# A fixed order for VectorE in the first strip, the weight quantised earlier, the second strip's keys and gates moved

## The chip, the cores and the metric

The kernel runs on one core of a Trainium2 chip. A core has a matrix engine (TensorE, PE), a vector engine (VectorE, DVE), an engine for functions such as exp (ScalarE, ACT), a general one (GpSimd, POOL) and one that only issues transfers and waits (SyncE, SP). Each runs its own queue strictly from front to back; an instruction that waits for a semaphore holds up all that is queued behind it. Tiles lie in SBUF (128 partitions), results of matmuls in PSUM. The metric is the device time of one execution in microseconds (us): less is better.

## What is computed

Two layers over 2 x 2048 tokens of 256 features. Layer 0, which the change touches, adds to x a gated linear attention with two heads and a linear map whose activations and weight are rounded to a six-bit grid in blocks of 32:

```python
xn = _layernorm(x)
v, q, lg = jnp.split(xn @ W_in.T, 3, axis=-1)
q = silu(q); k = 1.0 - sigmoid(lg); g = log_sigmoid(lg)
# per head, token by token:  S = exp(g)[:, None] * S + k[:, None] * v[None, :];  o = q @ S
o = o * sigmoid(xn @ W_g1.T @ W_g2.T)
attn = (o - mean(o)) * rsqrt(var(o) + 1e-5) * ln_w @ W_out.T
ffn = dequantised(xn) @ dequantised(weight).T + bias
x = x + attn + ffn
```

Layer 1 is an attention with 16 heads and a routed mixture of eight experts; its part of the program (some three quarters of the time) has almost the same order before and after.

## The kernel before

Layer 0 (`layer0`, L499 on) goes over the tokens in eight strips of 512, each held as four tiles of 128 tokens; strips 0 to 3 and 4 to 7 are the two sequences. A `Strip` has one method for each piece of work:

- `norm_x`: statistics (`LayerNorm.see`: `bn_stats` L119, `bn_aggr` L121), then `LayerNorm.apply`: the variance plus eps (L126), a power on GpSimd (L128), four scalings to `xn` (L130). GpSimd then adds the feed-forward bias to x (L613). There is one buffer of `xn` (`bufs=1`).
- `columns_x`: eight transposes on TensorE (L565) and two ScalarE copies to `xnT`.
- `values_gates`: `vf_ps` on TensorE (four tiles), for each a VectorE copy to `logit` (L633) and a ScalarE copy to `v` (L634), and for two tiles at a time `soft`, in two ScalarE steps.
- `queries`: `q_ps` and the cumulative gates `c_ps` on TensorE, `ls` on ScalarE, `arg` and `q` on VectorE (L680 to L683). `keys` (`k_ps`, `kt`), `gates` (`g1T`), `gates_end` (`gate`), `key_columns` (`k_tr`, `k`).
- `quantise`: the rounding of `xn`, in two halves of two tiles. Each half runs `mx_steps` (L149): nine operations on VectorE and then GpSimd (L191), VectorE (L193), GpSimd (L194), VectorE (L196), GpSimd (L197), each on the result of the one before. `quantised_columns` transposes the result (`mx_v` to `xdT`). `quantised_weight` does the same once for the weight `ffnw`, with four transposes (`wtr`).
- `weights` (`a_ps`, masked by VectorE at L757), then `chunk(0)` to `chunk(3)`: `o_ds_ps` on TensorE, the running state on VectorE and ScalarE (`sum` L796, `state` L799, `to_next` L792), `og` and its statistics.
- `norm_o`, `columns_o`, `sum_up` (`y_ps`), `norm_2`, `columns_2`, and `queries_keys`, `values`, `greatest` for the next layer.

The pieces of neighbouring strips are interleaved by hand in the loop at the end of `layer0` (L867 on): while strip s goes through its chunks, strip s+1 gets its values, queries, keys and gates, and strip s+2 is normalised.

The written order binds TensorE: every matmul and transpose of layer 0 goes through `tc.keep_in_program_order`, and instructions given to it stay on their engine in the order in which they were written. All others are placed by a scheduler at build time, among the pinned ones, by its own idea of when they are ready. On VectorE only two steps of `mx_steps` (L193, L196) are pinned, and for the weight none.

PSUM has six tiles under the name `mm` that `vf_ps`, `q_ps`, `c_ps`, `k_ps`, `g_ps`, `tr` and others share. SP issues the loads of x and constants in the written order, each also waiting until one of eight semaphores is free again; ScalarE's queue issues the loads of `wvf`, `wqT`, `sums`, `wg1T`, `wg2T` at the start.

## Time and profile before

Four runs have a median of 1774.44 us (1773.37 to 1775.82). One execution was profiled.

| | us |
|---|---|
| profiled execution, its own time | 1774.15 |
| its span in the profile | 1772.3 |
| TensorE busy | 1674.6 (94%) |
| VectorE busy | 694.4 (39%) |
| ScalarE busy | 803.4 (45%) |
| GpSimd busy | 395.8 (22%) |

The starts of `vf_ps`, the first matmuls of a strip's values, cut layer 0 into stages: 19.73 us for strip 0, then 48.76, 105.90, 156.97, 207.08, 256.4, 308.2 and 358.3. Attention begins at 453.8.

How to read the lines that follow. A row of the timeline has start, duration, engine, source line, operation, output and inputs, shapes, a count where several were merged, and in brackets how long the engine sat idle before it and what ended that. A row of waits has who waited, for whom, the total in us, how often, and the longest. A row of windows gives a stretch, its length, the busy time and number of instructions for TensorE's matmuls, its weight loads, VectorE, ScalarE and GpSimd, then the granted share of TensorE's clock, the share of the DMA engines and GB/s. A line number can be that of a helper: L565 are all transposes, L515 all matmuls of layer 0.

### The profile page before, as it was taken

What the parts mean: (1) busy time and instruction counts of PE and PEld (TensorE: products, weight loads), DVE (VectorE), ACT (ScalarE), POOL (GpSimd) and SP (SyncE); (2) the same over time, 40 slices, a digit from 0 to 9 for tenths busy, and PEclk for the clock granted to TensorE, in tenths of its full rate; (3) what the DMA queues carried; (4) which work ended last, traced back from release to release, by engine and by line L of the source; (5) the groups of instructions that cost most, each with busy time, mean ns of one, the idle gap of its engine ahead of it and who ended that gap; (6) DMA issues with size and microseconds to landing.
All of it is one profiled execution on the core that took longest, in us unless ns stands there. A gap on an engine that the chain in (4) does not pass through costs nothing.

```text
span 1772.3 us, 31816 instructions
## 1 busy us (share of the span) xinstructions
PE 1674.6 (94%) x13314; PEld 1298.1 (73%) x13314; DVE 694.4 (39%) x1798; ACT 803.4 (45%) x1590; POOL 395.8 (22%) x350
## 2 busy tenths in 40 slices
PE   5789999998999989999999999999999999999995
PEld 2467666666666656766666688898888888889885
DVE  7877767654554663242242222222222222222221
ACT  2345554453787767978988911111111111111110
POOL 4332222121200003333320012222222222222211
PEclk9899999999999999999999999999999999999998
DMA  9601113104610401351130175556555556557531
GB/s 250 171 23 39 50 50 91 59 24 104 139 13 1 77 13 60 90 116 60 54 136 14 38 271 172 164 174 214 177 179 185 183 183 195 164 176 238 164 84 17
DMA packets 82505, 204.33 MB, mean 115 GB/s; under 512 B 8624, under 2 KB 64304, under 8 KB 71728
## 3 DMA queue, kind: packets, MB, share of 16 engines
q0 software_dynamic: 24944, 138.33, 24.3%
q1 hardware_dynamic: 56304, 62.71, 13.7%
q8 instruction: 106, 1.74, 0.4%
q10 hardware_dynamic: 1104, 1.18, 0.2%
q14 instruction: 47, 0.39, 0.1%
HBM read 152.26 MB, written 49.92 MB: 114 GB/s over the span
## 4 chain that ended last, share of the span: by engine, by line
PE 82%; DVE 9%; ACT 5%; POOL 1%; DMA 1%; issue 1%; SPq 0%; POOLq 0%; DVEq 0%
PE h_ps L2113 27%; PE y_ps L2129 13%; PE sc L1687 11%; PE o_ps L1718 10%; PE qk_ps L515 3%; ACT pt L1693 3%; PE y_ps L515 3%; PE vf_ps L515 2%; PE f_ps L1670 2%; DVE pt L1705 2%; PE tr L565 2%; PE vg_ps L515 2%; PE g_ps L515 2%; PE o_tr L1644 1%; PE o_ds_ps L515 1%; PE x_ps L2091 1%
## 5 line engine op out<-in xcount | busy, mean ns | idle before, releaser
L1693 ACT ACTIVATE pt<-sc,shift 128x512 f32<-128x512 f32 (+3 forms) x832 | 463.9, 680 | 98.7 <-PE sc L1687 96.7
L2113 PE MATMUL h_ps<-va,qk 128*128 128x256 f32 (+1 forms) x2368 | 484.3, 365 | 0.0
L2113 PEld LDWEIGHTS h_ps<-va,qk 128*128 128x128 f32 x2368 | 425.4, 190 | 53.3 <-ACT va L2095 0.2
L2118 ACT ACTIVATE sg<-h_ps 128x256 f32<-128x256 f32 (+1 forms) x296 | 109.1, 369 | 593.8 <-PE h_ps L2113 575.9
L1687 PE MATMUL sc<-qk 32*128 32x256 f32 (+6 forms) x3680 | 276.4, 369 | 4.2 <-DVE onT L1664 1.7
L2119 DVE TENSOR_TENSOR larger<-sg,h_ps 128x256 f32<-128x256 f32 (+1 forms) x296 | 119.2, 403 | 355.4 <-ACT sg L2118 336.2
L1687 PEld LDWEIGHTS sc<-qk 32*128 32x128 f32 x3680 | 201.0, 185 | 62.8 <-ACT pt L1693 26.9
L1718 PE MATMUL o_ps<-pt,va 128*32 128x256 f32 (+7 forms) x3680 | 229.3, 352 | 17.5 <-DVE o_sb L1751 17.4
L1718 PEld LDWEIGHTS o_ps<-pt,va 128*32 128x32 f32 x3680 | 122.2, 110 | 96.9 <-issue 29.6
L2138 POOL DMA_INDIRECT out<-va,to x69 | 110.1, 1595 | 214.3 <-DVE larger L2119 59.3
L1705 DVE TENSOR_TENSOR pt<-pt,keepmask 128x1024 f32<-128x1024 f32 x64 | 78.3, 1224 | 184.8 <-ACT pt L1693 184.8
L2129 PE MATMUL y_ps<-qk,larger 128*128 128x256 f32 x560 | 124.3, 379 | 1.0 <-DVE va L2134 1.0
L2129 PE MATMUL y_ps<-larger 128*128 128x256 f32 x544 | 120.4, 379 | 0.0
L2129 PEld LDWEIGHTS y_ps<-qk,larger 128*128 128x128 f32 x560 | 104.8, 190 | 14.8 <-DVE va L2134 1.4
L2134 DVE SCALAR_TENSOR_TENSOR va<-y_ps,wt,half_bias 128x256 f32<-128x256 f32 x69 | 30.5, 480 | 209.8 <-PE y_ps L2129 209.8
L2129 PEld LDWEIGHTS y_ps<-larger 128*128 128x128 f32 x544 | 102.0, 190 | 13.1
L2023 POOL DMA_INDIRECT table<-rows,place x64 | 69.7, 1089 | 185.2 <-DMA table<-rows,place 147.1
L2053 POOL DMA_INDIRECT qk<-in_wgateup,wrow x37 | 37.3, 1009 | 284.1 <-PE h_ps L2113 150.3
L515 PE MATMUL vf_ps<-qk,xnT 128*128 128x512 f32 x128 | 58.8, 614 | 0.0
L515 PE MATMUL o_ds_ps<-state,q 128*128 128x128 f32 x120 | 26.1, 301 | 22.8 <-ACT state L799 22.8
L515 PEld LDWEIGHTS vf_ps<-qk,xnT 128*128 128x128 f32 x128 | 24.3, 195 | 29.3 <-issue 27.3
L1675 DVE TENSOR_TENSOR acc<-acc,f_ps 128x512 f32<-128x512 f32 x32 | 22.0, 687 | 56.8 <-PE f_ps L1670 54.1
(246 smaller groups left out, 1722.6 us busy)
## 6 DMA issues: line engine op xcount, KB each, us to landing
xb<-table SPq DMA_DIRECT2D x32, 265.0 KB
qk<-qk SPq DMA_DIRECT2D x32, 256.0 KB
qk<-qk SPq DMA_DIRECT2D x64, 128.0 KB
table<-spare SPq DMA_DIRECT2D x3, 2120.0 KB
va<-v SPq DMA_DIRECT2D x4, 1208.0 KB
v<-v SPq DMA_DIRECT2D x8, 574.0 KB
normed<-xn SPq DMA_DIRECT2D x8, 512.0 KB
rows<-normed POOLq DMA_DIRECT2D x16, 256.0 KB
```

Of the source, the lines that this page charges most:

```text
L515: tc.keep_in_program_order(nc.tensor.matmul(*args, **kwargs))
L1687: nc.tensor.matmul(scs[r][:, at : at + q1 - q0], lhsT=heads[rows, 1, kb * P : (kb + 1) * P], rhs=heads[rows, 0, qt * QT + q0 : qt * QT + q ...
L1693: nc.scalar.activation(pt[:, r, 0:width], scs[r][:, 0:width], AF.Exp, bias=shift)
L1705: ins = nc.vector.tensor_tensor(part, part, mask[:, 1 - way, :].unsqueeze(1).unsqueeze(1).to_broadcast([P, 4, 2, P]), ALU.min,)
L1718: nc.tensor.matmul(o_ps[r * HR : (r + 1) * HR, to + q0 : to + q1], lhsT=va[:, kb, h * VC : h * VC + HR], rhs=pt[:, r, at : at + q1 - q0], ...
L2023: self.nc.gpsimd.indirect_dma_start(out=self.c.table, in_=rows[:, n, :], in_offset=None, out_offset=bass.IndirectOffsetOnAxis(ap=to[:, 2 * ...
L2053: e.nc.gpsimd.indirect_dma_start(out=w, out_offset=None, in_=e.a[name], in_offset=bass.IndirectOffsetOnAxis(ap=e.c.wrow[:, self.b : self.b ...
L2113: nc.tensor.matmul(ps[:, j, rows], lhsT=self.wgu[:, j, c, f * P : (f + 1) * P], rhs=self.xT[:, c, rows], start=c == 0, stop=c == 1,)
L2118: nc.scalar.activation(sg, ps[:, 0, rows], AF.Silu)
L2119: nc.vector.tensor_tensor(self.hT[:, f, rows], sg, ps[:, 1, rows], ALU.mult)
L2129: nc.tensor.matmul(ps[:, c, :], lhsT=self.hT[:, fc, c * P : (c + 1) * P], rhs=self.wd[:, fc, :], start=fc == 0, stop=fc == NFC - 1,)
L2138: nc.gpsimd.indirect_dma_start(out=out, out_offset=bass.IndirectOffsetOnAxis(ap=self.to[:, c : c + 1], axis=0), in_=y[:, c, :], in_offset= ...
```

## The change

`see` and `mx_steps` can now pin their first operation too (`begin`), and so hold whole pieces in place on VectorE. The part ahead of the loop is written anew: strip 0's normalisation and columns, then the weight's rounding in two gaps, strip 1's normalisation, and the first half of strip 0's rounding, each between pieces of strip 0. The second half of strip 0's rounding and its transposes come behind `chunk(1)`; strip 1's keys and gates come before strip 0's output is transposed; strips 1 and 2 are pinned while strip 0 is worked on. The load of the weight goes ahead of strip 1's x on SP's queue. Three small VectorE operations that read late loads (`bq`, `own`, `bvb`) move to later places. `xn` gets a second buffer. From strip 1 on, the loop is written as before.

```diff
-    def see(self, src, first):
+    def see(self, src, first, begin=lambda ins: ins):
...
-            self.nc.vector.bn_stats(st[:, i, :], src[:, i, :])
+            begin(self.nc.vector.bn_stats(st[:, i, :], src[:, i, :]))
...
-def mx_steps(nc, pool, src, v, pin=lambda ins: ins):
+def mx_steps(nc, pool, src, v, pin=lambda ins: ins, begin=lambda ins: ins):
...
-    nc.vector.tensor_reduce(amax, blocks(x), AX.X, ALU.max, apply_absolute_value=True)
+    begin(nc.vector.tensor_reduce(amax, blocks(x), AX.X, ALU.max, apply_absolute_value=True))
...
-        nc.vector.tensor_copy(self.bvb, self.bv.unsqueeze(2).to_broadcast([P, 2, P]))
...
+    def prepare(self):
+        nc = self.nc
+        ins = nc.vector.tensor_scalar(self.bias[0], self.bias[0], HD**-0.5, None, ALU.mult)
+        self.tc.keep_in_program_order(ins)
+        self.own = self.pool.tile([P, HR], BF16, tag="own_bf", name="own_bf")
+        self.tc.keep_in_program_order(nc.vector.tensor_copy(self.own, self.own_f))
...
+    wq_nat = load("ffnw", early(2, E), rows("ffnw"), nc.sync)
     load_x(1)
...
-    wq_nat = load("ffnw", early(2, E), rows("ffnw"), nc.sync)
...
-        for _ in mx_steps(nc, p1, wq_nat, v):
-            pass
+        yield from mx_steps(nc, p1, wq_nat, v, pin, pin)
...
-            self.xn = p2.tile([P, 4, E], F32, tag="xn", name="xn", bufs=1)
+            self.xn = p2.tile([P, 4, E], F32, tag="xn", name="xn", bufs=2)
...
-    now = strips[0]
-    begin(now)
-    for piece in (now.values_gates, now.queries, now.gates, now.keys, now.gates_end,
-                  now.key_columns):
-        piece()
-    for _ in now.quantise():
-        pass
-    begin(strips[1])
+    now, weight = strips[0], quantised_weight()
+    quantise = now.quantise(begin=pin)
+    now.norm_x()
+    now.columns_x()
+    next(weight)
+    strips[1].norm_x(begin=pin)
+    now.values_gates()
+    next(weight)
+    now.queries()
+    next(weight)
+    now.gates()
+    now.keys()
+    next(quantise)
+    now.gates_end()
+    now.key_columns()
+    next(quantise)
+    strips[1].columns_x()
+    next(weight, None)
...
-        if not before:
-            now.quantised_columns()
-        quantise = after.quantise() if after else iter(())
+        if before:
+            quantise = after.quantise() if after else iter(())
         next(quantise, None)
         now.chunk(0)
         next(quantise, None)
         now.chunk(1)
+        if not before:
+            for _ in quantise:
+                pass
+            now.quantised_columns()
+            projections.prepare()
+            quantise = after.quantise(begin=pin)
...
-        if not before:
-            weight = quantised_weight()
-            next(weight)
         now.norm_o()
         if before:
             before.queries_keys()
+        else:
+            after.keys()
+            next(quantise)
+            after.gates()
+            for _ in quantise:
+                pass
         now.columns_o()
         if later:
-            later.norm_x()
-        if after:
+            later.norm_x(**({} if before else {"begin": pin}))
+        if before and after:
             after.keys()
-        if not before:
-            next(weight, None)
...
+        tc.keep_in_program_order(
+            nc.vector.tensor_copy(ready.bvb, ready.bv.unsqueeze(2).to_broadcast([P, 2, P]))
+        )
         ps = ps_m.tile([P, E], F32, tag="mm", name="b_ps")
```

## The prediction

> **What bounds the kernel now.** I read the page first. TensorE is busy for 94% of the span, and the chain that ended last lies on it for 82%, on VectorE for 9%:

> ```profile
> span 1772.3 us, 31816 instructions
> PE 82%; DVE 9%; ACT 5%; POOL 1%; DMA 1%; issue 1%; SPq 0%; POOLq 0%; DVEq 0%
> ```

> So only time in which TensorE waits, or runs at half clock, can be won. The waits of TensorE up to 105.9 us, where strip 2's values start (`vf_ps`), are the ones the change aims at:

> ```profile
> PE tr L565 <- DVE xn L130: 17.5, 1, 17.5
> PE tr L565 <- DVE og L130: 7.6, 4, 5.9
> PE o_ds_ps L515 <- ACT state L799: 5.2, 2, 4.0
> PE k_ps L515 <- DVE arg L680: 2.0, 1, 2.0
> PE y_ps L515 <- ACT wdT L596: 1.5, 1, 1.5
> PE c_ps L515 <- ACT soft L638: 1.4, 1, 1.4
> ```

> They come to 35 us (columns: total, times, longest). VectorE's rows in order of time say why the first is so long:

> ```profile
> 14.51 1.40 DVE L119 BATCH_NORM_STATS2 ln_stx<-acc 128x6 f32<-128x256 f32 x4 [3.31 <-DMA acc<-in_x]
> 16.98 0.17 DVE L437 TENSOR_SCALAR bq<-bq 128x2 f32<-128x2 f32 x1 [1.07 <-DMA bq<-in_bq]
> 17.05 1.06 DVE L130 TENSOR_SCALAR xn<-acc,ln_mvx,ln_rstdx 128x256 f32<-128x256 f32 x3
> 19.18 1.80 DVE L170 TENSOR_SCALAR mx_scale<-mx_amax 128x16 f32<-128x16 f32 x1
> ```

> The first normalisation stands behind strip 2's statistics and a bias whose transfers are late. The last row is 16 elements wide and takes 1.80 us: GpSimd's addition L613 ran from 18.60 for 2.36 us, and it ended with it. I charge such a block wherever a 512- or 1024-wide GpSimd operation meets a VectorE scaling, copy or product of SBUF tiles; in this trace statistics, reductions and reads of PSUM kept their time beside one. Last, windows of the length at which the clock is granted:

> ```profile
> 36.98:40.39 3.41, 1.41 (x6) 0.82 (x5) 3.41 (x8) 0.00 (x0) 1.55 (x2) 1.00 1.13 290
> 40.39:43.80 3.41, 3.41 (x8) 2.22 (x8) 3.41 (x10) 2.26 (x4) 1.05 (x1) 0.50 1.11 285
> 88.18:91.59 3.41, 1.88 (x10) 1.51 (x9) 3.41 (x18) 1.69 (x4) 0.70 (x2) 1.00 0.00 0
> ```

> (TensorE's busy time comes second, its clock third from the end.) A window 41% busy is followed by one at half clock; one 55% busy, by none. So a wait of about 1.8 us or more inside one window costs up to 1.7 us beyond itself. The half clock held from 71.1 to 88.2, and before 23.3.

> **The change, step by step.** The built order has as many instructions on each engine as before: nothing is added or removed but one buffer of `xn`. I went down the new order of each engine and gave each instruction the duration of its row in this trace and the end of what it waits for. The same sum over the old order gives 48.7, 107.8, 157.7, 207.2 and 255.8 us for the starts of `vf_ps` of strips 1 to 5, where the trace has 48.8, 105.9, 157.0, 207.1 and 256.4; so a point is good to about 1 us, 2 where a slow window falls differently.

> *Start.* `xn` now stands directly behind the GpSimd power that ends at 9.75; four rows of 0.33, and the transposes begin at 10.3, not 17.52: **-7.2**.

> *To strip 1's values.* The waits of 1.44 (`soft`) and 2.00 us (`arg`) go, and with them the slow window 40.39 to 43.80 (-1.7). The weight's four transposes come forward (+0.4), the keys' wait for ScalarE (+0.7). `vf_ps` of strip 1 starts at 36.6, not 48.76: **12.2 ahead**.

> *The new wait.* Strip 0's quantised columns moved behind chunk 1, and their second half is queued on VectorE behind the fourth `logit` copy, which waits for `vf_ps` and ends at 43.9. Then follow L196 to L188, nine rows with 4.6 us; three GpSimd rows (1.27, 1.27, 1.07) with two of VectorE between (0.69, 0.65) and hand-overs of 0.03 to 0.18 make 5.4; chunk work between them and one block, 1.6: ready at 55.5. TensorE has work only until 46.9. So it stands **8.7 us**, then runs two windows slow (+2.2), while the old wait of 4.05 for the state shrinks to 1.1. `q_ps` starts at 57.0, not 60.29: 3.3 ahead.

> *To strip 0's sum.* `og` transposes start at 74.5, not 79.69. Keys and gates of strip 1 lie before them and the weight's transposes are done, so the 3.4 us of `k_ps` at half clock, 0.9 of `wtr` and the wait of 1.53 no longer follow. `y_ps` starts at 77.7, not 89.90: **12.2 ahead**.

> *What is late next.* Statistics of six strips ran before 52 us, in VectorE's early room (24 rows L119); now two strips' do. The 16 moved rows (16 x 0.34 us) and their 16 aggregates (0.08) lie from 82 us on, with strip 2's `xn` ahead of strip 0's last normalisation. So TensorE waits 2.2 us for it behind the gates, and `vf_ps` of strip 2 starts at 98.3, not 105.90: **7.6 ahead** (y to there took 16.0, takes 20.6, 1.7 of it in a slow window).

> *Strips 1 to 3.* In strip 1 the fourth `logit` copy stands behind two `xn` rows that wait for a power of 1.02, and `arg` behind a reduction (0.67) and blocks: the state waits of 1.75 and 1.48 become 2.2 and 3.6 (+2.6), one more slow window (+1.7). In strips 2 and 3 the reduction L168 stands ahead of `arg`: 2.1 for 1.49, +0.6 each; at 2.1 us of wait I count half a slow window each, +0.85. Together **+7.2**. From strip 4 the order is almost the old one.

> **Sum: -7.6 + 7.2 = -0.4 us.** Against the profiled execution, 1774.15 us (span 1772.3), that is 1773.7; the median of 1774.44 lies 0.3 higher.

> *Costed at nothing, and the cover.* The weight's load (256 KB) passes strip 1's x on SP's queue and delays x, the feed-forward bias and the mask by some 1 us: x came at 9.30 and would at 10.2, and is read at 16.9 behind the weight's quantisation; the cover is 6 us; were x later than that, the `logit` copies queued behind it would wait, and TensorE too once the two free ones of its six PSUM tiles are full (`q_ps`, 3.4 us). The weight itself lands near 8.3 for 11.0. If late, VectorE stands, and strip 1's `xn` behind it, 13 us before its use. The scaled bias and `own` wait no more on the path: read at 54. `bvb` goes to attention, where VectorE is busy for 391 of 1332 us: a copy (1.13 us when blocked, 0.33 alone) with `b_ps` (0.86 us on TensorE) behind it; nothing if the copy is early, at most 1.1 if TensorE stands for it all; I take 0, VectorE being idle for seven tenths of that stage. Behind all this TensorE does the same work in the same order but for a few `o_ps`, so a shift carries to the end.

> [...] That a wait of 2 us drops the clock is the row's: 41% busy, then 0.50. [...]

> **Rivals.**
> - *Kept in full.* VectorE's later load hides beside TensorE in strips 1 to 3, as L168 and the statistics do from strip 4 on. For it: VectorE is busy for only 38.25 of 51.07 us in strip 1. Against: the waits there are for VectorE's order, not its load. -7.6, up to -9.5 if strip 2 starts earlier too: 1766.5 to 1764.6.
> - *Half kept.* The slow windows I added behind waits of 2.1 to 2.2 us (1.7 at 93 us, 1.7 in strips 2 and 3) don't come. -3.8: 1770.3. For it: the bound lies somewhere between 41 and 55% busy. Against: 2.00 us sufficed at 38 us.
> - *Slower, by the clock gate.* Each wait from 2.0 us up (at 75, 93, 109, 120, 172, 224 us) falls whole into one window and is followed by 3.41 us at half clock: 1.7 each. I counted three and two halves; all six, and a third window behind the 8.7 us wait, add 2 x 0.85 + 1.7 + 1.7 = 5.1: 1778.8. [...] Against: windows lie by chance.
> - *Does it do what it says?* The new order pins what the text names; that it then still waits 8.7 us for the quantised columns is part of the forecast.

> **How the numbers follow.** Used up, as summed, within 2.5 us: 0.60, likeliest time 1773.7. Kept in full 0.14, half kept 0.12, slower 0.14. A measurement of this kernel tells 0.2% from none, 3.5 us: the likeliest case lies within it nearly whole (0.57 of 0.60). Faster: 0.14 + 0.07 of the half-kept case + 0.02 = 0.23; slower: 0.12 + 0.01 = 0.13; within: 0.64. The range takes in the likeliest case (1771.2 to 1776.2), the half-kept and the slower case short of its worst, and stops short of the case kept in full: 1767.5 to 1778.0.

> **What would show it.** Right: `tr` at 10.3; `vf_ps` of strip 1 near 36.6; a wait of 8 to 9 us of `tr` for GpSimd's `mx_v` near 47; `y_ps` near 77.7; strip 2 near 98, strip 5 within 2 us of 256.4; waits for the state of 2 us and more in strips 1 to 3. Wrong: `tr` at 55 ready sooner, or strips 1 to 3 at the old 51.07, 50.11 and 49.32 us: then it is faster. Strips over 54, 52 and 52 with more than five slow windows after 50 us: slower.

## The result, and the profile after

The changed kernel takes 1777.65 us in the median of 32 runs (1775.91 to 1780.37) against 1774.38 us before (52 runs): a ratio of 1.0017, 95% interval 1.0012 to 1.0021. It is slower, by 3.3 us, where no change (-0.4 us) was forecast. The profiled execution has a span of 1777.2 us, 4.9 more than before. Its page begins as before, with the chain of waits on TensorE:

```profile
span 1777.2 us, 31814 instructions
PE 83%; DVE 8%; ACT 5%; POOL 1%; issue 1%; DMA 1%; SPq 0%; POOLq 0%; DVEq 0%; ACTq 0%
```

The waits of TensorE up to 105.9 us (who, for whom, total, times, longest):

```profile
PE tr L568 <- DVE xn L130: 10.1, 1, 10.1
PE tr L568 <- POOL mx_v L197: 8.3, 1, 8.3
PE tr L568 <- DVE og L130: 3.7, 3, 3.1
PE tr L568 <- ACT gate L723: 2.0, 1, 2.0
PE o_ds_ps L518 <- ACT state L802: 1.6, 2, 1.0
PE k_tr L736 <- ACT kt L704: 0.5, 1, 0.5
```

The first wait fell from 17.5 to 10.1 us, those for `soft`, `arg` and `wdT` are gone, and the forecast new one, for GpSimd's `mx_v`, is there with 8.3 us. So the early strips went as forecast. The loss must lie elsewhere, and a table finds it by cutting the span at the first score product of attention (`sc`) and at the end of the last matmul. The cuts are read from the timelines, the differences worked out:

| us | attention begins | from there to TensorE's end | from there to the span's end |
|---|---|---|---|
| before | 453.77 | 1301.24 | 17.26 |
| changed | 453.84 | 1308.00 | 15.34 |
| difference | +0.07 | +6.76 | -1.92 |

Layer 0, which the change was about, ends where it ended. The loss is in attention, where the change moved a single VectorE copy, of the constant `bvb` that the product `b_ps` reads. TensorE's and VectorE's rows there, in order of time (start, duration, engine, line, operation; in brackets the idle time before and what ended it):

```profile
598.54 0.39 PE L1503 MATMUL sk_ps<-sk_c,ones_mat 128*128 128x8 f32 x2
598.86 1.49 PE L1738 MATMUL o_ps<-pt,va 128*32 128x192 f32 x22
...
600.39 0.69 DVE L1771 COPY o_sb<-o_ps 128x512 f32<-128x512 f32 x1 [1.22 <-PE o_ps L1738]
601.00 0.42 DVE L1476 TENSOR_TENSOR pi<-pi,sk_by 128x256 f32<-128x256 f32 x1
...
602.17 0.10 DVE L1506 TENSOR_TENSOR grown<-grown,sk_most 128x1 f32<-128x1 f32 x1
602.18 0.28 DVE L1596 COPY bvb<-bv 128x256 f32<-128x256 f32 x1
...
602.62 1.10 PE L1600 MATMUL b_ps<-cwf,bvb 128*128 128x256 f32 x4 [2.26 <-DVE bvb L1596]
...
605.82 0.69 ACT L1713 ACTIVATE pt<-sc,shift 128x512 f32<-128x512 f32 x1 [7.38 <-PE sc L1707]
```

The copy takes 0.28 us and waits for no transfer. But it is pinned, and stands on VectorE behind the copy of `o_sb`, which waits for the product `o_ps`, and behind six routing steps. `b_ps` stands directly behind that same `o_ps` on TensorE, so TensorE has nothing from 600.35 to 602.62. ScalarE, with no scores to work on, is idle for 7.38 us. Then windows of 3.41 us: in both profiles every stretch of half or full clock between two changes is a whole multiple of that (half clock lasts 3.41, 6.83, 10.24 or 17.07 us there). TensorE's busy time comes second, its clock third from the end:

```profile
600.25:603.66 3.41, 1.15 (x8) 0.69 (x7) 3.06 (x11) 0.00 (x0) 0.00 (x0) 1.00 0.63 153
603.66:607.07 3.41, 3.01 (x31) 2.41 (x31) 0.71 (x2) 1.25 (x3) 0.00 (x0) 0.50 1.30 298
607.07:610.49 3.42, 3.42 (x26) 2.70 (x18) 1.99 (x2) 3.13 (x8) 0.00 (x0) 0.50 1.03 122
610.49:613.90 3.41, 3.41 (x27) 1.96 (x26) 1.91 (x4) 1.91 (x4) 0.00 (x0) 0.50 0.99 130
613.90:617.31 3.41, 3.12 (x58) 2.42 (x58) 3.39 (x14) 2.25 (x4) 0.00 (x0) 1.00 0.81 87
```

The wait left the first window 34% busy, and three windows at half clock follow. Before, `b_ps` waited for nothing, score products followed it at once, and the same stretch ran at 1.00 throughout:

```profile
598.72 1.11 PE L1580 MATMUL b_ps<-cwf,bvb 128*128 128x256 f32 x4
599.76 1.15 PE L1687 MATMUL sc<-qk 32*128 32x256 f32 x16
600.18:603.59 3.41, 3.41 (x59) 2.54 (x52) 1.91 (x8) 2.60 (x5) 0.00 (x0) 1.00 0.01 2
603.59:607.00 3.41, 3.04 (x36) 1.95 (x34) 2.81 (x3) 3.41 (x8) 0.00 (x0) 1.00 0.83 211
```

TensorE is busy for 9.84 us in the three slow windows. In layer 0 of this profile the weight loads of `qk_ps` follow each other at 0.85 us under half clock (174.90 to 176.60) and at 0.43 under full (from 177.23). If all of the 9.84 us takes twice as long in the same way, that costs 4.9 us by estimate, and with the wait 7.2; TensorE's waits for `o_sb` in the stage are 1.4 us shorter, its other waits 0.9 longer, which leaves some 6.7 of the 6.76.

### The profile page after: what moved, and what is told of

The parts are those of the page before. It is cut to its first block, busy times and chain, and to the rows that moved or that the text cites. A ratio compares the mean times of both kernels' runs of the same rounds, so it can differ in the third digit from the quotient of the medians.

```text
span 1777.2 us, 31814 instructions
## 1 busy us (share of the span) xinstructions
PE 1684.9 (95%) x13314; PEld 1304.5 (73%) x13314; DVE 684.8 (39%) x1798; ACT 804.6 (45%) x1590; POOL 390.1 (22%) x350
## 3 DMA queue, kind: packets, MB, share of 16 engines
q8 instruction: 107, 1.75, 0.4%
## 4 chain that ended last, share of the span: by engine, by line
PE 83%; DVE 8%; ACT 5%; POOL 1%; issue 1%; DMA 1%; SPq 0%; POOLq 0%; DVEq 0%; ACTq 0%
PE h_ps L2133 27%; PE y_ps L2149 13%; PE sc L1707 11%; PE o_ps L1738 10%; PE y_ps L518 3%; ACT pt L1713 3%; PE qk_ps L518 3%; PE vf_ps L518 3%; PE tr L568 2%; PE f_ps L1690 2%; DVE pt L1725 2%; PE vg_ps L518 2%; PE g_ps L518 1%; PE o_tr L1664 1%; PE o_ds_ps L518 1%; PE a_ps L518 1%
## 5 line engine op out<-in xcount | busy, mean ns | idle before, releaser
L2158 POOL DMA_INDIRECT out<-va,to x69 | 110.1, 1595 | 215.4 <-DVE larger L2139 71.1
L2043 POOL DMA_INDIRECT table<-rows,place x64 | 65.9, 1030 | 181.8 <-DMA table<-rows,place 142.9
```

Of the source, the lines that this page charges most:

```text
L2043: self.nc.gpsimd.indirect_dma_start(out=self.c.table, in_=rows[:, n, :], in_offset=None, out_offset=bass.IndirectOffsetOnAxis(ap=to[:, 2 * ...
L2158: nc.gpsimd.indirect_dma_start(out=out, out_offset=bass.IndirectOffsetOnAxis(ap=self.to[:, c : c + 1], axis=0), in_=y[:, c, :], in_offset= ...
```

## The experiments

Each states its theories' numbers ahead. Medians are of 6 to 12 runs, beside the kernel before on the same chip (1774.2 to 1775.2).

### The copy: undone, moved, alone

The copy put back to the load of the constants, unpinned, with all else as changed:

```diff
         nc.sync.dma_start(out=self.bf, in_=a["bf"].unsqueeze(0).to_broadcast([P, E]))
+        nc.vector.tensor_copy(self.bvb, self.bv.unsqueeze(2).to_broadcast([P, 2, P]))
...
     def value_bias():
-        tc.keep_in_program_order(
-            nc.vector.tensor_copy(ready.bvb, ready.bv.unsqueeze(2).to_broadcast([P, 2, P]))
-        )
```

> The changed kernel with one part undone: the copy to bvb is again where the constants are loaded, unpinned, and the scheduler places it on VectorE near 51 us, in strip 0's chunks. Theory (the copy's late place is the whole loss): b_ps no longer waits (2.26 us gone) and none of the three half-clock windows from 603.7 to 613.9 follows; layer 0 ends as in the changed kernel (attention at 453.8 within 0.5, up to 1 later if the copy is blocked or its load is late), so 1774 to 1775, equal to the kernel before within 0.1%. Rival (the three slow windows fall there for another reason, the wait being only 2.3 us of the 4.9): 1775.5 to 1776 with slow windows still near 604. Rival (the loss lies elsewhere): 1777.6.

1772.31 us, ratio to before 0.9988 (0.9978 to 0.9998). The copy ran at 51.5 us in 0.28 us, and `b_ps` waited for nothing. Second, the same pinned copy at the start of attention, ahead of its units:

```diff
+    tc.keep_in_program_order(
+        nc.vector.tensor_copy(ready.bvb, ready.bv.unsqueeze(2).to_broadcast([P, 2, P]))
+    )
     experts = Experts(tc, a, out, c, rooms, blocks)
```

> The changed kernel with the copy to bvb pinned at the start of attention (near 454 us) and not in front of b_ps. Theory: as with the copy placed by the scheduler, no wait at b_ps near 599 to 603, 1774 to 1775; the copy itself costs 0.3 us of VectorE where TensorE has work. Rival (a pinned copy in attention costs in any place): 1776 or more.

1770.75 us, ratio 0.9977 (0.9968 to 0.9987). It ran at 453.7 us. Attention begins at 453.85, as in the changed kernel, and takes 1301.11 us to TensorE's end, not 1308.00: between these two profiles, 6.9 us for the place of one copy. Third, the other way round, the kernel before with the late copy alone (L348 removed, the pinned copy put ahead of `b_ps`):

> The kernel before with only this part of the change: the copy to bvb taken from the constants' load and pinned directly in front of b_ps. Theory: layer 0 as before within 0.5 us, b_ps waits 2 to 2.5 us for bvb and TensorE then runs up to three windows at half clock: 1777 to 1779, that is the whole loss of the changed kernel alone. Rival (the loss needs the rest of the change, or the place of clock windows that its layer 0 sets): 1774.4 to 1775.5.

1780.51 us, ratio 1.0030 (1.0019 to 1.0040): 6.2 us slower than before, 1.5 us above the expected range, without any other part of the change, and with attention beginning at 453.91 as before. Its timeline shows the same wait, to the hundredth:

```profile
600.90 1.49 PE L1720 MATMUL o_ps<-pt,va 128*32 128x192 f32 x22
604.65 1.10 PE L1582 MATMUL b_ps<-cwf,bvb 128*128 128x256 f32 x4 [2.26 <-DVE bvb L1578]
```

Three windows at half clock follow here too, from 606 to 616. Fourth, the pinned copy left in its step (as `value_bias_copy`), but the product one step of attention later:

```diff
         if n == len(units) // 4:
+            value_bias_copy()
+        if n == len(units) // 4 + 1:
             value_bias()
```

> The changed kernel with the pinned copy to bvb where it is (behind the copy of o_sb on VectorE), but the product b_ps one attention step later in TensorE's order. Theory (TensorE's wait, and the clock behind it, cost the time, not the copy's place on VectorE): the wait at b_ps is under 0.3 us, no three half-clock windows behind it: 1774 to 1775. Rival (VectorE's changed order there, o_sb ahead of the routing steps, costs the time): 1777 or more.

1771.13 us, ratio 0.9978 (0.9969 to 0.9987). TensorE's and VectorE's rows in its timeline:

```profile
597.17 1.07 PE L1740 MATMUL o_ps<-pt,va 128*32 128x192 f32 x16
597.64 0.28 DVE L1594 COPY bvb<-bv 128x256 f32<-128x256 f32 x1
598.17 1.13 PE L1602 MATMUL b_ps<-cwf,bvb 128*128 128x256 f32 x4
```

TensorE has other products until `bvb` is there, and no wait and no slow windows come. The scheduler moved the copy of `o_sb` behind `bvb` too, so this run alone doesn't part TensorE's wait from VectorE's order; that the place on VectorE matters only through TensorE's wait is read from the rows above, not from this run. Together the four settle the loss: it goes in all three versions whose product doesn't wait for the copy, and comes with the late copy alone. The three came out 1.7 to 3.3 us below the 1774 to 1775 that was expected of them: that the copy is the whole loss was right, that the rest of the change is worth nothing was not. With the copy elsewhere, it is worth -2.0 to -3.6 us against before.

### The wait for the quantised columns

The base of this and the following runs, but for the early start alone, is the version with the copy at attention's start. In the first, strip 0's transposes of `mx_v`, which waited 8.3 us, come behind strip 1's queries and chunk 2:

```diff
-            now.quantised_columns()
             projections.prepare()
-            quantise = after.quantise(begin=pin)
-        next(quantise, None)
+        if before:
+            next(quantise, None)
         if after:
             after.queries()
         now.chunk(2)
+        if not before:
+            now.quantised_columns()
+            quantise = after.quantise(begin=pin)
+            next(quantise, None)
```

> The changed kernel with the copy to bvb at attention's start (the version that took 1770.75 us), and strip 0's quantised columns (the transposes of mx_v) moved from behind chunk 1 to behind strip 1's queries and chunk 2; strip 1's quantisation starts behind them. Theory (the 8.3 us wait of these transposes for GpSimd's mx_v, and the two half-clock windows behind it, stand on the path): the wait falls to 2 to 3 us, y_ps starts near 68 and not 78, strip 2's vf_ps near 92 and not 98.3; of this 6 us some 1.5 are lost again where strip 1's quantised columns come later (a wait of some 3 us near 81): 1766 to 1767.5. Rival (VectorE's work is the limit to strip 2, the wait only shows where it is waited for): strip 2 at 97 or later, 1769.5 to 1771.

1768.26 us, ratio 0.9967 (0.9955 to 0.9979), between the two expected ranges; the trace decides. `y_ps` starts at 68.01 and strip 2's `vf_ps` at 91.42, as the theory had it. Its waits up to 98 us:

```profile
PE tr L568 <- DVE xn L130: 11.2, 2, 10.1
PE tr L568 <- POOL mx_v L197: 4.9, 2, 3.1
```

Of 6.9 us won by strip 2, strip 3's start at 148.53 against 152.91 still shows 4.4: in strip 1 a longer state wait (4.35 us, 3.2 without the edit) and the window at half clock that follows it, 115.0 to 118.4, took most of the rest. The median kept 2.5. In the second, strip 2's normalisation also goes into the gaps of strip 1's rounding, and strip 1's quantised columns behind strip 2's:

```diff
             after.gates()
+            later.norm_x(begin=pin)
             for _ in quantise:
                 pass
         now.columns_o()
-        if later:
-            later.norm_x(**({} if before else {"begin": pin}))
+        if later and before:
+            later.norm_x()
...
-            after.quantised_columns()
             if before:
+                after.quantised_columns()
                 after.gates()
...
             after.gates_end()
+        if not before:
+            after.quantised_columns()
```

> As the run with the columns behind chunk 2, and besides: strip 2's normalisation goes on VectorE between the two halves of strip 1's quantisation, where VectorE waits for GpSimd, and strip 1's quantised columns come behind strip 2's. Theory (what is late next is strip 2's normalisation and strip 1's quantisation, both for their place in VectorE's order): strip 2's vf_ps near 91.5, strip 3's near 146 and not 152.9, strip 5's near 247 and not 256.6: 1762 to 1764. Rival (the waits of strips 1 to 3 stay whatever the place): 1766 to 1767.5, as without this.

1765.07 us, ratio 0.9947 (0.9934 to 0.9961): faster than both kernels, by 9.2 and 12.6 us, and 1 us above the expected range. Strip 2 starts at 91.30, strip 3 at 145.11, strip 5 at 245.86, attention at 441.87, 11.9 us ahead of before. Of these only 7.3 reach its profile's end, as the last section shows.

### The other parts

Strip 2's statistics no more pinned (`later.norm_x()` for all strips):

> The version that took 1770.75 us (changed kernel, copy to bvb at attention's start) with strip 2's statistics no more pinned behind strip 0's output, so that the scheduler may place them early, as before. Theory (the later statistics cost time in strips 1 to 3): strip 1's vf_ps some 2.8 later (39.4), strip 2's equal (98), but strip 3's near 150.5 and not 152.9: 1767.5 to 1769.5. Rival (strips 1 to 3 lose for the reduction's place ahead of arg alone): 1771 to 1773.5, the later start of strip 1 coming through.

1769.35 us, ratio 0.9969 (0.9957 to 0.9981). Strip 1 starts later (38.78), strip 2 equally (98.10) and strip 3 earlier (149.46, not 152.91): the later statistics do cost time in strip 1, 3.5 us in the profile. The median kept 1.4, which is hardly clear of the noise: the two versions' intervals, this one and 0.9968 to 0.9987, overlap. Its waits for the state are 1.48 and 2.12 us, 2.14 and 3.25 in the changed kernel. The early start alone, in the kernel before (`prepare` behind chunk 1, and `begin=` of strip 2's statistics as in the change):

> The kernel before with the early start alone: bq and own are scaled and copied behind chunk 1, and strip 2's statistics pinned behind strip 0's output, so that the first xn does not wait for their loads; nothing else of the change. Theory (a gain in strip 0 is taken back where VectorE's statistics are then late): tr starts near 12.7 and not 17.5, strip 1's vf_ps at 44 to 45 and not 48.8, strip 2's near 101 and not 106, but from strip 3 on within 1 us of before: 1773 to 1775. Rival (a shift of the first transposes carries to the end): 1769 to 1770.

1772.83 us, ratio 0.9991 (0.9982 to 1.0000). The transposes start at 12.24 and strip 2 at 99.38, 6.5 ahead; strip 3 starts at 155.61, 1.3 ahead of its 156.90, strip 5 at 255.08, also 1.3 ahead. Five of the 6.5 us are taken back in strip 1 alone, by a wait for the state of 4.72 us (1.75 before) and two windows at half clock behind it, 111 to 118 us. The time is a little below the expected range, and the strips lie 1.3 ahead where within 1 was expected: the mechanism held, and some 1.4 us were kept, by an interval that reaches to none. Strip 1's keys and gates back behind strip 0's output:

```diff
         else:
-            after.keys()
-            next(quantise)
-            after.gates()
             for _ in quantise:
                 pass
...
-        if before and after:
+        if after:
             after.keys()
...
-            if before:
-                after.gates()
+            after.gates()
```

> The version that took 1770.75 us (changed kernel, copy to bvb at attention's start) with strip 1's keys and gates back in their old places behind strip 0's output transposes and quantised columns. Theory (they fill TensorE's wait for strip 0's last normalisation, 3.1 us with them ahead of it): the wait for og grows to about 7 us, y_ps starts near 81 and not 78, and strip 2's and 3's waits for the state grow too: 1773 to 1776. Rival (the wait is filled anyway, only the place changes): 1770 to 1772.

1775.52 us, ratio 1.0002 (0.9992 to 1.0012). The wait for `og` grew from 3.1 to 6.5 us, `y_ps` starts at 80.79, and the waits for the state in strip 1 reach 5.29 and 3.87. Last, the weight's rounding back behind chunk 3 (its `next(weight)` calls moved there, the transposes ahead of `sum_up`):

> The same version with the weight's rounding (the four pieces, still pinned) back behind chunk 3 of strip 0 and its transposes ahead of y_ps. Theory (VectorE and GpSimd have no room left there, since the statistics and strip 1's rounding now lie there too): strip 1's vf_ps 1.2 us earlier (35.4), but the transposes wtr wait 10 to 14 us near 78 to 92, strip 2's vf_ps at 110 or later and not 98.3: 1777 to 1782. Rival (the scheduler's room behind strip 0's chunks still covers it, as in the kernel before, where wtr waited for nothing and y_ps 1.5 us): 1770 to 1772.

1781.85 us, ratio 1.0038 (1.0025 to 1.0050). Its waits up to 112 us name the place:

```profile
PE wtr L597 <- POOL wd L197: 13.9, 1, 13.9
```

So each of these two parts is worth its place, by the ratios 0.25% (4.4 us) for keys and gates and 0.61% (10.8 us) for the weight, in the surroundings that the rest of the change made.

## Why the prediction was wrong

*What bounds the kernel, and layer 0: right in its steps, with some luck in the sum.* The forecast start of each step beside the trace:

| us | forecast | trace |
|---|---|---|
| first transposes | 10.3 | 10.09 |
| strip 1 `vf_ps` | 36.6 | 36.63 |
| new wait for `mx_v` | 8.7 | 8.3 |
| `q_ps` of strip 1 | 57.0 | 57.03 |
| `og` transposes | 74.5 | 74.83 |
| `y_ps` | 77.7 | 77.94 |
| strip 2 `vf_ps` | 98.3 | 98.21 |
| state waits, strip 1 | 2.2, 3.6 | 2.14, 3.25 |
| state waits, strips 2 and 3 | 2.1, 2.1 | 2.11, 2.11 |
| end of layer 0 against before | -0.4 | +0.07 |

Three things the table doesn't show. The terms listed for strip 1's values and for strip 0's sum come to 11.2 and 11.0 us, where the prediction has 12.2 ahead twice and the trace 12.13 and 11.96: some 1 us of each has no term. The 2.0 us ahead of the transposes of strip 0's last normalisation ended with ScalarE's `gate` at 93.22, and `xn`, which was named, was ready 0.13 us sooner. And the slow window counted for strip 1 (1.7) did not come, while the two counted half in strips 2 and 3 came whole (0.85 more each): that 7.9 us were measured for the three strips where +7.2 was forecast is in part luck, since these nearly cancel.

That the late statistics take back part of the gain is shown by the run that leaves them unpinned (some 3.5 of the 7.9 us), and that the wait for the quantised columns lies on the path to strip 2 by the run that moves them; the rest, by the reduction's place ahead of `arg`, was not tried by itself.

*The step that failed: "nothing if the copy is early, at most 1.1 if TensorE stands for it all; I take 0, VectorE being idle for seven tenths of that stage".* Its late place cost 5.3 to 6.9 us, by which of the three versions without it is compared, and 6.2 in the kernel before. Two things are wrong in the step. The bound was the copy's own duration. But the copy, pinned directly ahead of its reader, cost what stood ahead of it in VectorE's queue: the copy of `o_sb`, itself waiting for the matmuls that TensorE has just done, and the chain behind it, 2.26 us for a copy of 0.28. A stage's mean idleness says nothing of that. And windows at half clock behind a wait, which the prediction counted everywhere in layer 0, were not counted here, where there were three, two thirds of the cost by the estimate above (4.9 of 7.2 us). Row by row, the order around the copy showed it: `o_ps`, then `b_ps` on TensorE; `o_sb`, six routing steps, then `bvb` on VectorE.

*"So a shift carries to the end": wrong in part.* It holds for the changed kernel, which ends layer 0 at the same time as before, but not in general (last section).

*The rivals.* "Half kept", that slow windows behind waits of 2.1 us may not come, was seen: the run with the product one step later has the changed kernel's layer 0 and the same waits, and ends it at 449.12, not 453.84. Strip 2's wait of 2.11 us, in the windows of the changed kernel first:

```profile
170.17:173.59 3.42, 1.31 (x11) 1.12 (x11) 3.19 (x11) 1.74 (x4) 0.24 (x1) 1.00 0.00 0
173.59:177.00 3.41, 3.41 (x8) 1.80 (x7) 2.97 (x7) 0.69 (x2) 1.26 (x1) 0.50 0.00 0
```

and of that run, where the border of two windows falls into the wait:

```profile
167.76:171.17 3.41, 2.34 (x21) 2.15 (x20) 3.28 (x10) 0.99 (x4) 1.31 (x2) 1.00 0.00 0
171.17:174.58 3.41, 2.37 (x13) 1.79 (x14) 3.03 (x8) 1.77 (x6) 0.00 (x0) 1.00 0.00 0
174.58:178.00 3.42, 3.42 (x9) 1.52 (x8) 2.67 (x7) 2.42 (x5) 1.92 (x2) 1.00 0.20 77
```

38% busy is followed by half clock, 69% twice by none: behind waits of 2.11 us a window at half clock came in the one profile and not in the other, by where the wait fell, as argued. What such a window costs, 1.7 us, is an estimate, half of its 3.41. But the bound "somewhere between 41 and 55% busy" doesn't hold. In the changed kernel the window 91.65 to 95.06, 53% busy, is followed by half clock, and 115.54 to 118.96, 52% busy, is not; and at attention's start, in the run with the product one step later, even a window that is 93% busy is followed by half clock:

```profile
451.07:454.48 3.41, 3.18 (x30) 2.12 (x31) 2.46 (x6) 3.41 (x9) 2.27 (x2) 1.00 0.82 222
454.48:457.89 3.41, 3.41 (x41) 1.94 (x40) 2.32 (x2) 2.27 (x4) 3.41 (x2) 0.50 1.06 306
```

In the profiles of the changed layer 0 (the changed kernel and the first, second and fourth runs) attention begins at 453.84, 450.99, 453.85 and 449.12, 451.95 in the mean, against 453.77 before and 453.91 with the late copy alone. The four spread over 4.7 us with the same order in layer 0 but for that copy, so about -1.8 for layer 0 is an estimate; the +0.07 of the table is one execution, and its closeness to the -0.4 says little. The slower rival, 1778.8, came near the measured time by another cause; of its six places four had slow windows behind them in the changed kernel (75, 93, 172 and 224 us), 109 and 120 none.

*The sum, as measured.* Medians, with the copy at attention's start: the copy +6.9 (1777.65 less 1770.75), all else -3.6 (1770.75 less 1774.30); with the copy placed by the scheduler it is +5.3 and -2.0. How the rest divides is not shown: the mean of the four profiles would give layer 0 about -1.8, but in the profile of the copy at attention's start layer 0 is worth nothing, and the 1.9 us lie at the end of the program, which no step had foreseen. The range reached to 1778.0 and held the time only because of the slower rival, not because of this cost.

## What to carry to other kernels

An operation moved next to its reader must be priced by all that stands ahead of it in its own queue at the new place, waits included (here 2.26 us for a copy of 0.28), and not by its duration or by how idle the engine is in the mean; a small constant is best prepared long before its use. Where TensorE binds, look for windows at half clock behind its waits and count them too, in every stage and not only in the one that the change is about: here there was one behind waits of 2.00 us (at 38 us before the change) and 2.11 us (at 172 us in the changed kernel), three behind 2.26 us at `b_ps`, and none behind 2.11 us at 172 us with the product one step later. A gain at the front was taken back here where VectorE's work was only put off: look for what is late next, and give it a place in the gaps of another chain, as strip 2's normalisation got between the rounding's steps (3.2 us in the medians; with the columns moved and the copy early, 9.2 us faster than before).

## What the runs showed of the hardware

- After the wait at `b_ps` the clock came back only after three windows, though the second was busy for all of its 3.42 us; in the changed kernel's layer 0, it was back behind one full window each time (57.5 to 60.9, 78.0 to 81.4, 173.6 to 177.0 us). Both kernels with the late copy show three. One difference is in the rows: the full window behind which the clock was not back, 607.07 to 610.49, held only `sc` products of the form 32*128, that of 173.6 only products of the form 128*128. Whether that is what counts was not tried.
- The same attention and experts took different times from profile to profile (one of each kernel). From the first score product to TensorE's end the kernels without the late copy need 1301.1 to 1301.3 us in four (before, the copy at attention's start, the columns behind chunk 2, the weight back), 1303.2 to 1303.5 in two and 1306.6 to 1307.1 in four. The four slowest have two or three windows at half clock at attention's start (446 to 453 us in the fastest version, 453 to 463 with the copy placed by the scheduler) and one more some 80 us behind it, the two between one at the start, the four fastest neither. So some 5 us of what layer 0 wins can be lost there. That it depends on where attention begins in the grid of windows is a likely reading, and was not tested by itself.
- From TensorE's last matmul to the end of the span it takes 17.3 and 17.9 us in the kernel before and in that with the late copy alone, 16.4 with the early start alone, and 15.3 to 16.5 in all kernels made from the changed one, with the same work there. In the kernel before, GpSimd's last but one scatter starts 1.02 us after the row it writes is ready, with nothing in the profile that it waits for; in the changed kernel 0.30 us. The cause is open.
